# PSUM banks of layer 0 in a four-batch transformer kernel: three for the first keys and values, one for the second int8 block

## The chip, the cores and the metric

The kernel runs on one core of a Trainium2 chip as one launch. The metric is the device time of that launch in microseconds. The core has five engines, each with its own in-order instruction queue: TensorE (PE), VectorE (DVE), ScalarE (ACT), GpSimd (POOL) and SyncE (SP). Matrix products land in PSUM, which this kernel cuts into eight banks, "bank0" to "bank7", each one tile of 128 partitions by 512 float32 values.

## The reference, cut to what matters

The input `x` has 4 batches of 512 rows by 512 columns. Four residual steps follow one another; layer 0 is the first two:

```
x = x + tanh(g_xattn[0]) * L0_xattn(layernorm(x), fside, ctx)     # int8 block
x = x + tanh(g_ffn[0])   * L0_ffn(layernorm(x), w_fc, w_proj)     # ternary block
x = x + tanh(g_xattn[1]) * L1_xattn(layernorm(x), ctx, mask, Wq, Wk, Wv, Wo)
x = x + tanh(g_ffn[1])   * L1_ffn(layernorm(x), router_w, norm_w, gate_w, up_w, down_w)
```

The int8 block is a small expert network for each batch, with both its products in a smoothed int8 form:

```
s   = sqrt(max(amax_x, EPS) / max(amax_w, EPS))    # amax per column
x_q = round((x / s) / x_scale), w_q = round((w * s) / w_scale)    # scale per row: max / 127
out = x_q @ w_q.T * x_scale * w_scale.T
h   = smooth_quant_linear(xe, guw);  a = silu(gate) * up;  y = smooth_quant_linear(a, dw)
```

The ternary block is `square(relu(x @ sign(w_fc).T)) @ sign(w_proj).T`, scaled by the mean sizes of the weights, where the signs are taken against a threshold. The attention of layer 1 needs keys and values, `ctx @ Wk` and `ctx @ Wv`, of every batch. They depend on nothing that layer 0 computes, so they can be worked out at any time before.

## The kernel before, in words

All of layer 0 lies in one block of code. The batches are staged like this, in program order: `int8_block(0)`; the means of the ternary weights (`mean_of`); `int8_block(1)`; the signs of the ternary weights (`load_signs`, 22 pieces of which each takes two DVE passes, a transpose on PE and a copy on ACT); `keys_values_of(0)` and `keys_values_of(1)`; `ternary_in(0)`; then for each batch `ternary_block(b)`, with `int8_block(b + 1)` put in at high priority while batches 1 and 2 are in the ternary block, and `keys_values_of(2)` after batch 0's ternary block and `keys_values_of(3)` at the end. This program order is not the order of execution. A scheduler sorts the instructions of each engine by priority and by when it thinks they can start, and what it makes is fixed: every engine then works its list strictly in order. The tag of a tile (here a bank) is another order: the users of one bank follow one another as in the program, whatever their priorities.

The steps that matter here, by their lines:

- `int8_block` (from layer norm on): `column_max` transposes the activations, four 128x128 pieces to a bank (L198), and DVE reduces the bank (L251); four banks for the first product, two for the second. A scale per column follows (L294 and the square root L151 to L158, L296, L298), is turned into rows by PE (L204), copied by ACT (L300), and multiplied in by DVE (L303, activations) and POOL (L305, weights). `quantize` takes row maxima (L275), scales (L281), transposes (L198) and ACT copies each bank out (L283); DVE clips (L284). Then four products of the first matrix (L336), each read by DVE (L340), SiLU (L341) and a product on POOL (L342). The second half does all of this again on half the columns (`weight_max` L264 and L266, then L198 to L284), with four products L350, each read by DVE (L358) and added to the residual by POOL (L359). The maxima of the weights come first of all, by a DVE reduction (L259).
- Every one of those PSUM tiles comes from `home()`, which goes round the banks of `HOMES` for this batch: banks 4 and 5 for batch 0, 6 and 0 for batch 1, bank 0 alone for batches 2 and 3.
- `keys_values` transposes the context (L495, copied by L496), then makes 16 products of 128x512 with two matmuls each (L501). ACT copies each product to one of two staging places (L503), and SP stores it to memory (L504). Its banks are 7 and 3 in turn for batches 0 and 1, and 3 alone for batches 2 and 3.
- `ternary_in` normalises on ACT (L180), transposes (L436) and splits into two parts (L439 on ACT, L440 on DVE). Its tile `xn` shares a ring of two with the tiles `h` and `y` of the int8 blocks.
- `ternary_block` makes 160 matmuls with the first weights (L462) and 160 with the second (L449, into banks 4 to 7), with the two passes L470 and L472 on ACT, L473 on POOL and L474 on DVE between them. Banks 1 and 2 (`turn_bank`) serve the first products, the signs and the transposes.

Of the kernel before, what the change touches and what calls it, by code (L numbers as in the profile page):

```python
# [57 lines left out]
def kernel(  # L58
# [71 lines left out]
    def bank(i, dtype=F32):  # L130

        return bank_p.tile([P, 512], dtype, tag=f"bank{i}", name=f"bank{i}")
# [77 lines left out]
    with tc.tile_pool(name="q8", bufs=1) as q8, tc.tile_pool(name="l0", bufs=2) as l0, tc.tile_pool(  # L210
# [4 lines left out]
        def next_of(what, n):  # L215
            turns[what] += 1
            return turns[what] % n
# [4 lines left out]

        HOMES = ((4, 5), (6, 0), (0,), (0,))
        xlast = X[B - 1].rearrange("p t k -> p (t k)")
        first_room = (place_in(dn, SLOT + 4096, 512), place_in(dn, SLOT + 4608, 1024))
        rooms = [
# [11 lines left out]
        def home():  # L240
            mine = HOMES[now[0]]
            return bank(mine[next_of("home", len(mine))])
# [240 lines left out]
        def load_context(b, queue):  # L483
            at = SLOT + 2048 if b in (0, B - 1) else SLOT
            cr = place_in(dn, at, NT * DC).rearrange("p (t k) -> p t k", t=NT)
            queue.dma_start(cr, rows(cvec[b]))
            return cr

        def keys_values(b, place, cr):

            cT = place_in(dn, SLOT + 1024, KC * S).rearrange("p (k s) -> p k s", k=KC)
            for i in range(KC):
                tp = place()
                for t in range(NT):
                    nc.tensor.transpose(tp[:, t * P : (t + 1) * P], cr[:, t, i * P : (i + 1) * P], ident)  # L495
                nc.scalar.copy(cT[:, i, :], tp)  # L496

            def product(dst, lhs, rhs):
                ps = place()
                for i in range(KC):  # L500
                    nc.tensor.matmul(ps, lhsT=lhs(i), rhs=rhs(i), start=(i == 0), stop=(i == KC - 1))  # L501
                st = place_in(dn, SLOT + 2048 + 512 * next_of("kvs", 2), 512)
                nc.scalar.copy(st, ps)  # L503
                nc.sync.dma_start(dst, st)  # L504

            for j in range(NKV):
                product(
                    kd[b][j * HD : (j + 1) * HD, :],
                    lambda i: wkv[0][:, i, j * HD : (j + 1) * HD],
                    lambda i: cT[:, i, :],  # L510
                )
            for t in range(NT):
                for c in range(0, NKV * HD, 512):
                    product(
                        vd[b][t * P : (t + 1) * P, c : c + 512],
                        lambda i: cT[:, i, t * P : (t + 1) * P],
                        lambda i: wkv[1][:, i, c : c + 512],
                    )
# [8 lines left out]
        fs1 = load_rows(1, nc.gpsimd)  # L527

        def keys_values_of(b):
            places = (7, 3) if b < 2 else (3,)  # L530
            context = load_context(b, nc.sync) if b else ctx0
            keys_values(b, lambda: bank(places[next_of("kv", len(places))]), context)

# [7 lines left out]
        load_signs(w_fc, fcT, NH, KD, fc_thr, held)  # L541
        load_signs(w_proj, pjT, KD, NH, pj_thr)
        keys_values_of(0)
        keys_values_of(1)
        xT = ternary_in(0)
        for b in range(B):
            if 0 < b and b + 1 < B:
                with tc.high_priority(offset=2000):
                    int8_block(b + 1, load_rows(b + 1), load_cross(b + 1))
            ternary_block(b, xT)  # L550
            if b + 1 < B:
                with tc.high_priority(offset=0):
                    xT = ternary_in(b + 1)
            if b == 0:
                keys_values_of(2)
# [562 lines left out]
    for i in range(LAST + 3):  # L1118
        b, n = divmod(i, NHEAD)
# [199 lines left out]
```

## Time and profile before

| | us |
|---|---|
| median of 3 runs (lowest to highest) | 1570.09 (1568.76 to 1570.95) |
| the profiled execution, its own time | 1567.48 |
| its span, first to last instruction | 1565.7 |
| PE, DVE, ACT, POOL busy in the span | 1475.8, 905.0, 554.0, 414.0 |
| first instruction of the first ternary block (L462) | 164.26 after the start of the span |
| PE busy in 0 to 164.26 | 128.43 |
| PE busy in 164.26 to 440 | 255.78 of 275.74 |
| mean granted TensorE clock | 0.988 |

The span leaves out about 1.8 us of the profiled execution's own time. All times inside the kernel are given from the start of the span. The first 440 us or so are layer 0; the rest is attention and the routed experts. In the timeline a line has the start, the length, the engine, the line of the kernel, the operation, output and input with shapes, the number of instructions merged into the line, and in brackets how long the engine was idle before and what released it. One float32 matmul of the program shows as two records on PE, and one keys-or-values product as four.

### The profile page before, as it was taken

How to read it: one execution, taken by the hardware profiler on the slowest of the kernel's cores; microseconds unless marked ns; L12 is line 12 of the kernel's file. 1: busy time of each engine (PE TensorE's matmuls, PEld its weight loads, DVE VectorE, ACT ScalarE, POOL GpSimd, SP SyncE). 2: the span in 40 equal slices, each digit the busy share in tenths (PEclk: the TensorE clock that was granted, in tenths of full speed). 3: DMA queues.
4: the chain of work that ended last, by engine and by line, in shares of the span. 5: the costliest groups of instructions: out<-in, count | busy, mean ns of one | idle time of the engine just before them, and what ended most of it. 6: DMA issues, size and time to landing. Idle time of an engine off the chain costs nothing. (4 is left out here: it accounts for less than half of the span.)

```text
span 1565.7 us, 15898 instructions
## 1 busy us (share of the span) xinstructions
PE 1475.8 (94%) x4294; PEld 740.9 (47%) x4294; DVE 905.0 (58%) x2339; ACT 554.0 (35%) x1141; POOL 414.0 (26%) x540
## 2 busy tenths in 40 slices
PE   4988998899999999999999999999999998899995
PEld 2454656666544444444444444444444443455553
DVE  5898737556275555586565675665668553653320
ACT  3554453444243333253323353333433331412111
POOL 2232314352311113131131141141141111335422
PEclk9999999999999999999999999999999999999998
DMA  8633111013355445475455485475584653567542
GB/s 300 222 116 129 47 41 62 28 41 97 126 160 150 133 138 157 136 218 153 127 151 141 129 223 149 117 187 143 153 233 127 159 146 99 149 115 144 122 89 38
DMA packets 110840, 211.10 MB, mean 135 GB/s; under 512 B 28816, under 2 KB 32912, under 8 KB 110752
## 3 DMA queue, kind: packets, MB, share of 16 engines
q0 software_dynamic: 32736, 97.73, 24.0%
q1 hardware_dynamic: 70224, 100.74, 22.9%
q10 hardware_dynamic: 7792, 11.60, 2.1%
q8 instruction: 37, 0.61, 0.2%
q14 instruction: 51, 0.42, 0.1%
HBM read 95.34 MB, written 34.93 MB: 83 GB/s over the span
## 5 line engine op out<-in xcount | busy, mean ns | idle before, releaser
L674 DVE CUSTOM_DVE_ANT_0 e<-bank,mask_b 128x512 f32<-128x512 f32 x256 | 175.0, 688 | 245.7 <-PE bank L669 245.6
L694 PE MATMUL bank<-eT,v 128*128 128x512 f32 x512 | 230.5, 592 | 2.2 <-DVE nmax L674 2.2
L669 PE MATMUL bank<-kT,qT 128*128 128x512 f32 x512 | 231.1, 593 | 0.0
L708 PE MATMUL bank<-wo,oT 128*128 128x512 f32 x512 | 230.7, 592 | 0.3 <-ACT oT L698 0.3
L677 ACT ACTIVATE e<-e,nmax 128x512 f32<-128x512 f32 x256 | 184.3, 720 | 81.6 <-DVE nmax L674 74.5
L571 DVE STREAM_TRANSPOSE blocks<-e 128x512 f32<-128x512 f32 x256 | 158.9, 677 | 30.7 <-DMA eT<-blocks 26.1
L656 PE MATMUL bank<-gu,wq 128*128 128x512 f32 x384 | 174.9, 594 | 1.2 <-DVE nmax L674 1.2
L694 PEld LDWEIGHTS bank<-eT,v 128*128 128x128 f32 x512 | 97.1, 190 | 125.4 <-issue 109.3
L669 PEld LDWEIGHTS bank<-kT,qT 128*128 128x128 f32 x512 | 97.0, 190 | 123.1 <-issue 114.8
L708 PEld LDWEIGHTS bank<-wo,oT 128*128 128x128 f32 x512 | 97.1, 190 | 122.7 <-issue 120.1
L698 ACT COPY oT<-bank 128x512 f32<-128x512 f32 x64 | 37.4, 584 | 315.9 <-PE bank L694 298.4
L656 PEld LDWEIGHTS bank<-gu,wq 128*128 128x128 f32 x384 | 72.3, 190 | 91.9 <-issue 82.3
L635 POOL DMA_DIRECT2D wq<-in_L_xattn_Wq_dram x64 | 48.5, 758 | 245.8 <-PE bank L656 223.7
L685 DVE TENSOR_SCALAR e<-e,rt 128x512 f32<-128x512 f32 x256 | 108.2, 485 | 2.1
L650 POOL DMA_DIRECT2D wo<-in_L_xattn_Wo_dram x64 | 36.5, 571 | 266.9 <-PE bank L708 260.7
L660 ACT ACTIVATE qT<-bank 128x512 f32<-128x512 f32 x64 | 38.2, 597 | 171.6 <-PE bank L656 165.7
L449 PE MATMUL bank<-pjT,hT 128*128 128x512 f32 x320 | 86.4, 405 | 5.4 <-DVE hT L474 5.4
L462 PE MATMUL bank<-xfT,fcT 128*128 128x512 f32 x320 | 89.8, 410 | 0.0
L1093 PE MATMUL bank<-gu,turned 128*128 x192 | 86.5, 593 | 0.0
L501 PE MATMUL bank<-dn,gu 128*128 128x512 f32 x128 | 68.9, 655 | 10.5 <-ACT dn L503 5.0
L473 POOL TENSOR_TENSOR r<-r 128x512 f32<-128x512 f32 x40 | 41.7, 1044 | 107.8 <-ACT hT L472 83.5
L1093 PEld LDWEIGHTS bank<-gu,turned 128*128 128x128 f32 x192 | 56.4, 295 | 28.0 <-issue 5.7
(361 smaller groups left out, 1896.8 us busy)
## 6 DMA issues: line engine op xcount, KB each, us to landing
eT<-blocks SPq DMA_DIRECT2D x1016, 64.0 KB, 2.6
wq<-in_L_xattn_Wq_dram POOLq DMA_DIRECT2D x64, 256.0 KB, 3.8
wo<-in_L_xattn_Wo_dram POOLq DMA_DIRECT2D x64, 256.0 KB, 3.0
kd<-dn SPq DMA_DIRECT2D x32, 256.0 KB, 2.0
vd<-dn SPq DMA_DIRECT2D x32, 256.0 KB, 2.0
kT<-kd POOLq DMA_DIRECT2D x32, 256.0 KB, 3.6
v<-vd POOLq DMA_DIRECT2D x32, 256.0 KB, 4.1
turned<-blocks SPq DMA_DIRECT2D x96, 64.0 KB, 3.5
```

What stands on the lines that cost most here:

```text
L449: nc.tensor.matmul(outs[t], lhsT=h[:, t * P : (t + 1) * P], rhs=pjT[:, j, :], start=(j == 0 and u == 0), stop=(j == NH - 1 and u == 1),)
L462: nc.tensor.matmul(ps, lhsT=fcT[:, i, j * P : (j + 1) * P], rhs=xT[u][:, i, :], start=(u == 0 and i == 0), stop=(u == 1 and i == KD - 1),)
L501: nc.tensor.matmul(ps, lhsT=lhs(i), rhs=rhs(i), start=(i == 0), stop=(i == KC - 1))
L571: nc.vector.transpose(blocks[:, :, :, t, :].rearrange("p c s r -> p s c r"), src.rearrange("p (s c i) -> p s c i", c=NQ, i=Q))
L656: nc.tensor.matmul(ps, lhsT=th[:, i, :], rhs=xT[:, :, i, :], start=(i == 0), stop=(i == KD - 1))
L669: nc.tensor.matmul(ps, lhsT=qT[:, t * P : (t + 1) * P], rhs=kT, start=True, stop=True)
L674: nc.vector.tensor_tensor_reduce(e, ps, mask_b[b], -1.0, 3.0e38, ALU.add, ALU.min, nmax[:, t : t + 1])
L677: nc.scalar.activation(e, e, AF.Exp, bias=nmax[:, t : t + 1], scale=-1.0, accum_out=total[:, t : t + 1])
L685: nc.vector.tensor_scalar(es[:, t, :], es[:, t, :], rt[:, t : t + 1], None, ALU.mult)
L694: nc.tensor.matmul(ps, lhsT=v[:, s, :], rhs=eT[:, :, s, :], start=(s == 0), stop=(s == NT - 1))
L708: nc.tensor.matmul(sums[b][t], lhsT=oT[:, t * P : (t + 1) * P], rhs=to, start=(n == 0), stop=(n == NHEAD - 1))
L1093: nc.tensor.matmul(ps, lhsT=xgT[k], rhs=gu[:, bass.ds(e, 1), k, :], start=(k == 0), stop=(k == KD - 1))
```

## The change

Two lines. The second int8 block (batch 1) keeps bank 6 and gives up bank 0, so that each of its PSUM tiles waits until the one before it has been read. The keys and values of batches 0 and 1 go round the banks 7, 3 and 0. Batches 2 and 3 are as before in both places.

```diff
-        HOMES = ((4, 5), (6, 0), (0,), (0,))
+        HOMES = ((4, 5), (6,), (0,), (0,))
...
         def keys_values_of(b):
-            places = (7, 3) if b < 2 else (3,)
+            places = (7, 3, 0) if b < 2 else (3,)
             context = load_context(b, nc.sync) if b else ctx0
             keys_values(b, lambda: bank(places[next_of("kv", len(places))]), context)
```

No instruction is added to the arithmetic or taken from it. The scheduler, which sees other waits, puts the lists of PE, DVE, ACT, POOL and SP in another order up to the end of layer 0. Before the first L462 on PE there are now 92 matmuls of line L501 where there were 79; the counts of the int8 blocks, the signs and `ternary_in(0)` before it are the same. On ACT two more loads of an activation table stand in that stretch (another L151 and another L341).

## The prediction

> **What bounds the kernel now.** I read the page's busy slices first, then busy time by stage, then the instruction timeline around the stage where the ternary blocks start, then the waits of PE, and last the built instruction lists of both programs. From the page:
>
> ```profile
> PE   4988998899999999999999999999999998899995
> DVE  5898737556275555586565675665668553653320
> ```
>
> A slice is 39.1 us. From the fifth slice on PE is the full engine and DVE is half idle: there, time is PE work plus PE's gaps. In slices 2 to 4 DVE is as full as PE. By stage (length; busy time and records of PE, PEld, DVE, ACT, POOL; clock, DMA share, GB/s):
>
> ```profile
> 20.00:60.00 40.00, 33.23 (x122) 17.64 (x123) 33.23 (x78) 23.64 (x52) 13.06 (x27) 0.91 0.75 258
> 60.00:100.00 40.00, 37.34 (x165) 19.53 (x164) 38.68 (x79) 19.72 (x37) 13.79 (x14) 1.00 0.47 165
> 100.00:140.00 40.00, 33.25 (x160) 17.75 (x159) 34.81 (x76) 22.86 (x44) 9.98 (x12) 0.96 0.35 126
> 140.00:164.26 24.26, 20.63 (x78) 10.08 (x77) 18.98 (x48) 11.54 (x22) 5.14 (x5) 1.00 0.37 131
> 164.26:440.00 275.74, 255.78 (x1074) 171.76 (x1073) 152.64 (x342) 111.26 (x197) 97.15 (x110) 0.99 0.20 64
> ```
>
> Between 20 and 164.26 PE is idle 144.3 - 124.5 = 19.8 us and DVE 144.3 - 125.7 = 18.6 us. What ends this stage is read from the timeline:
>
> ```profile
> 154.68 0.73 DVE L358 SCALAR_TENSOR_TENSOR y<-bank,gsc,xlast 128x512 f32<-128x512 f32 x1
> 155.50 1.27 POOL L359 TENSOR_TENSOR gu<-gu,y 128x512 f32<-128x512 f32 x1 [2.19 <-DVE fs_am L267]
> 156.80 0.81 ACT L180 ACTIVATE xn<-gu,ln_d,ln_rstd 128x512 f32<-128x512 f32 x1 [2.14 <-POOL gu L359]
> 164.26 3.08 PE L462 MATMUL bank<-xfT,fcT 128*128 128x512 f32 x11
> ```
>
> The last y of int8 block 1 releases a buffer on POOL, ACT waits for it (xn shares the ring), and 7.5 us after the second xn the ternary block starts. So **the end of int8 block 1 sets when the PE-bound part begins**; keys and values only fill PE before it.
>
> **The change, part by part.**
>
> *The third bank of keys and values.* Its worth is what PE waits there. PE's waits from 20 to 138 us, where keys and values 0 and 1 lie:
>
> ```profile
> PE bank L264 <- DVE dn L259: 3.4, 1, 3.4
> ...
> PE bank L501 <- ACT dn L503: 1.3, 1, 1.3
> ```
>
> The Trainium skill (page "Perfetto Trace Analysis", section "Matmuls") says that independent matmul groups should rotate through PSUM banks so that emptying one overlaps the next group. Taken by that rule the 32 products would have 32 copies of 0.585 us (L503's mean) to hide, 18.7 us; by the row at most 1.3 us is left unhidden by two banks. The row decides: 0 to 1.3 us. The same rule speaks against the other half of the change, and there the rows agree with it (below). Two staging places and one ACT copy per product stay as they are, so products do not come faster than these.
>
> *What moves.* In the lists of the changed program 92 L501 matmuls instead of 79 stand before the first L462. Thirteen at 1.02 us (two records in the timeline, 1.02 each time) are 13.3 us of PE work taken out of the PE-bound part. If the first L462 kept its time, the kernel would be 13.3 us faster; it breaks even if L462 comes 13.3 us later, at 177.6. On SP the loads of batch 3 (fside L316, context L323, x L318) move behind four to seven more stores; nothing reads them before those products are made, so I take 0, with one exception in step 4. Behind the waiting L316 three stores are queued, and through the two staging places ACT's next copies: they cover two products, so 0 to 2 us, taken as 0. POOL's list has the same order up to the first L473.
>
> *The one bank of block 1.* The nearest row is block 2, which has one bank already, against block 1 with two, in the ACT copies L283:
>
> ```profile
> 111.45 1.13 ACT L283 ACTIVATE wT<-bank 128x512 bf16<-128x512 f32 x2
> 113.43 1.08 ACT L283 ACTIVATE wT<-bank 128x512 bf16<-128x512 f32 x2 [0.37 <-PE bank L198]
> 198.73 0.60 ACT L283 ACTIVATE wT<-bank 128x512 bf16<-128x512 f32 x1 [0.75 <-PE bank L198]
> 200.09 0.60 ACT L283 ACTIVATE wT<-bank 128x512 bf16<-128x512 f32 x1 [0.77 <-PE bank L198]
> ```
>
> With one bank a copy comes every 1.36 to 1.7 us, (201.47 - 191.19)/7 = 1.47; with two, eight take 7.0 us. Behind each now stands whatever L501 half the list has next (1.02). Following block 1 down the new DVE list with durations of this trace, its own places against before:
>
> 1. Column maxima: four L251, each waiting for the transpose of a bank that the one before it frees, with L414 and L417 between: up_q (L294) about 81 instead of 75.1, +6.
> 2. The row copy L300 of block 1 (before at 80.12) now stands on ACT behind block 0's L283s and L311, near 94. POOL's L305 of block 1 (4.95 us for four) runs 95 to 100, and block 0's L359 is behind it; block 0's third y on DVE waits for that L359 (ring of two), about 4 us with all of DVE's list behind it. Then the L303s, L275 (2.28 twice), L259 (1.93) and eight L281: the last L281 ends near 117 instead of 107.3, +10.
> 3. Eight L283 on one bank with L501 halves between: the clip L284 of wT at about 131 instead of 114.8, +16. The sign passes cover this on DVE; they are used up by it.
> 4. Four L336 and L340 on one bank. The list puts block 3's L259, 3.69 us in this trace, between the first and the second L340. Its load waits on SP until block 1's wT is transposed, so it may be later still. First L340 near 134 (116.8), fourth near 143.6 (124.3), +19.
> 5. The second half took 125.0 to 154.7, 29.7 us. Taken out: sign passes 5.3 us and an L259 of 3.7. Put in: 0.9 for the second L251, 0.8 for the second row, about 4 for four L283, 3 for four L350/L358 ("PE bank L350 <- DVE y L358: 3.2" is block 2's wait for the same), and L501 halves in front, some 4 us. About 33: last y near 177, +22.
>
> Then 7.5 to 8 us as before: the first L462 near 186, +22. The two extra table loads on ACT (1.28 us each in this trace) fall inside step 4 and 5 waits: 0 to 2.6, taken as 0.
>
> *What is late next.* PE-bound time loses 13.3 us of L501 that filled 212 to 240 us:
>
> ```profile
> 180.00:200.00 20.00, 0.00 (x0) 0.00 (x0) 1.00 0.00 0
> 220.00:240.00 20.00, 14.03 (x28) 4.67 (x28) 1.00 0.24 92
> ```
>
> (L501 alone, PE busy first.) At 212 to 224 they stand beside ternary_in(1), where L462 of batch 1 waits for xT until 219.8; with four halves, two L336 groups and the transposes left, PE stays covered there. Later, ternary block 1 is 13 us shorter while int8 blocks 2 and 3 keep their latency on bank 0, so PE can wait at the ends of ternary blocks 1 and 2, as it does now at 287.6 ("PE bank L449 <- DVE hT L474: 5.4, 3, 3.7"). In the new list keys and values 3 fill the second of these. I take +2, between 0 and 6.
>
> **Sum.** +22 - 13.3 + 2 = about +10 (the third bank's 1.3 is inside the rounding). Against the profiled execution's own 1567.5 (span 1565.7 and 1.8 around it) that is 1577.5; this execution is 2.6 below the median 1570.1, so against the median it is 1580.
>
> Bounds: step by step the +22 could be 14 (an L501 half in front of each block-1 step overlaps its wait fully in steps 3 and 5, -8) or 27 (block 3's L259 held by its load, POOL order worse, +5); the moved work is worth 10 to 13.3; the later gaps 0 to 6. That gives +1 to +20 or so around +10.
>
> **The rivals.**
>
> - *Faster: the first L462 slips less than the work that was put before it.* PE has 19.8 us of idle before 164.26, room for 13.3. Mechanism: block 1's longer waits are all inside the DVE idle (18.6 us) and the sign passes, so the chain above is shorter than counted one by one. It decides at 177.6: with L462 at 171 the kernel is 171 - 164.3 - 13.3 = -6.6, 1563.5. For it: the sum of work before L462 is the same on DVE. Against: steps 2 and 4 put DVE itself in waits with its list blocked behind. Chance 0.16.
> - *No difference.* L462 between about 174 and 181 with nothing lost later: 1570. That also covers the case that one bank costs little because block 1 is already spaced by DVE. Chance 0.12.
> - *Slower as worked out*, 1573 to 1588: chance 0.60.
> - *Slower by more*: the fill for the ends of the ternary blocks is gone and block 3's tail on bank 0 comes to stand before ternary_in(3); another 8 us, 1588 and above. For it: the new list puts block 3's last part behind the last L449 of ternary block 2. Against: keys and values 3 lie beside it. Chance 0.12.
> - That the change does not do what it says, for the keys and values: most likely true in effect; at the same place in the list they are one product ahead. It is part of all cases.
>
> **The numbers.** Slower by over 0.2% (3.1 us, about what a measurement of this kernel can tell from no change) 0.72, within 0.12, faster 0.16. The likeliest is 1580. The range 1568 to 1593 leaves out most of the faster case and the far end of the last.
>
> **What would show it.** After: L462 first near 186 and above 177.6; 26 more L501 records before it; the four L340 of block 1 with an L259 of 3.7 us among them, the fourth near 143; L283 of block 1 one at a time, 1.5 us or more apart; an idle of about 4 us on DVE before an L358 with POOL L359 as releaser near 100; L501 waiting for L503 before 138 for under 1.3 us. I am wrong if the first L462 is before 174, or if PE's idle between it and 440 falls by several us instead of rising.

## The result, and the profile after

The changed kernel takes 1576.94 us (median of 9 runs, 1572.42 to 1578.66); the kernel before, run beside it on the same chip, takes 1567.55 us (9 runs). The ratio is 1.0060, 95% interval 1.0045 to 1.0074: the change costs about 9.4 us. The prediction was +10 us, 1580.

The busy slices of the page, after. The slices are now 39.4 us long:

```profile
PE   5888899898999999999999999999999998899995
DVE  5786656766265556585565575665668552553220
```

The two kernels differ mainly in slices 2 to 5. The same by stage, after, with the boundary at its own first L462 (columns as for before: length; busy time and records of PE, PEld, DVE, ACT, POOL; granted clock, DMA share, GB/s):

```profile
20.00:60.00 40.00, 31.81 (x100) 16.46 (x100) 29.48 (x62) 20.81 (x46) 12.71 (x26) 0.91 0.70 249
60.00:100.00 40.00, 36.68 (x185) 20.82 (x187) 35.92 (x89) 22.99 (x45) 12.14 (x14) 1.00 0.46 161
100.00:140.00 40.00, 33.42 (x143) 17.77 (x143) 33.94 (x61) 20.92 (x39) 6.95 (x8) 0.88 0.42 139
140.00:184.59 44.59, 36.10 (x118) 15.97 (x117) 25.37 (x72) 20.06 (x35) 9.26 (x10) 0.99 0.31 112
184.59:440.00 255.41, 233.38 (x1019) 163.37 (x1024) 147.33 (x320) 102.81 (x179) 93.80 (x107) 0.99 0.17 56
```

From 20 us to the first L462, DVE is now idle 164.6 - 124.7 = 39.9 us where it was idle 18.6: it waits longer, it does not work longer. PE does 13.6 us more there, the thirteen L501 that its list had added, and is idle 26.6 us instead of 19.8.

The timeline of after, along block 1's path:

```profile
82.59 0.16 DVE L294 SCALAR_TENSOR_TENSOR up_q<-up_am,fs_am 128x4 f32<-128x4 f32 x1
...
100.54 0.75 DVE L358 SCALAR_TENSOR_TENSOR y<-bank,gsc,dn 128x512 f32<-128x512 f32 x1 [2.94 <-POOL gu L359]
...
133.01 3.70 DVE L259 TENSOR_REDUCE dn<-gu 128x512 f32<-128x2048 f32 x1
...
139.46 0.75 DVE L340 SCALAR_TENSOR_TENSOR h<-bank,upa_sc,xlast 128x512 f32<-128x512 f32 x1 [1.89 <-PE bank L336]
...
175.88 0.73 DVE L358 SCALAR_TENSOR_TENSOR y<-bank,gsc,xlast 128x512 f32<-128x512 f32 x1
...
184.59 2.36 PE L462 MATMUL bank<-xfT,fcT 128*128 128x512 f32 x9
```

The last y of block 1 starts 21.2 us later than before (154.68) and the first L462 20.3 us later (164.26). Why the steps between are slow shows in ACT's timeline of after, with three of block 1's copies (L283) on its single bank:

```profile
122.05 0.60 ACT L283 ACTIVATE wT<-bank 128x512 bf16<-128x512 f32 x1 [0.40 <-PE bank L198]
...
123.23 0.59 ACT L503 COPY dn<-bank 128x512 f32<-128x512 f32 x1
123.72 0.60 ACT L283 ACTIVATE wT<-bank 128x512 bf16<-128x512 f32 x1
...
125.09 0.60 ACT L283 ACTIVATE wT<-bank 128x512 bf16<-128x512 f32 x1 [0.51 <-PE bank L198]
```

A copy of 0.60 us comes every 1.3 to 1.9 us (one gap of 2.3 us aside). Before, they came in pairs of 1.1 us. The next transposes may start only when the copy has emptied the bank, but PE does not stand idle for it; its list has other work there:

```profile
122.08 1.08 PE L501 MATMUL bank<-gu,dn 128*128 128x512 f32 x2
122.99 0.60 PE L198 MATMUL bank<-ident,gu 128*128 128x128 f32 x4
123.43 0.28 PE L422 MATMUL bank<-ident_b,dn 128*128 128x128 bf16 x2
123.54 1.08 PE L501 MATMUL bank<-gu,dn 128*128 128x512 f32 x2
124.45 0.60 PE L198 MATMUL bank<-ident,gu 128*128 128x128 f32 x4
```

Before, two banks of transposes followed each other (eight pieces in a line):

```profile
109.29 1.04 PE L198 MATMUL bank<-ident,dn 128*128 128x128 f32 x8
...
110.68 1.15 PE L198 MATMUL bank<-ident,gu 128*128 128x128 f32 x8
```

With one bank the transposes at 122.99 and 124.45 have the copy of 123.72 to 124.32 between them, and an L501 fills the time. In the seven gaps of these eight copies the next transposes start 0.06 to 0.86 us after the copy has ended, 2.7 us in all: about so much the filler can have added here, and the rest is the way of a group through its bank. From block 1's last L281 (the end of its first scaling) to its last y, PE is busy 53.2 of 62.0 us after and 42.2 of 48.0 us before, with 35 L501 in the stretch instead of 25: the longer stretch is mostly filled, not idle.

How 20.3 us at the first L462 become 10.6 us at the end of the span, from the starts of L462 and of layer 1's queries (L656) in both traces. The L501 matmuls of a stretch are counted in PE's lists, before to after:

| stretch | before, us | after, us | difference | L501 in it |
|---|---|---|---|---|
| up to the first L462 | 164.3 | 184.6 | +20.3 | 79 to 92 |
| first to last L462 (ternary blocks) | 235.8 | 230.7 | -5.1 | 31 to 25 |
| to the first L656 | 10.1 | 9.2 | -0.9 | 4 to 3 |
| first to last L656 | 874.2 | 867.6 | -6.6 | 14 to 8 |
| to the end | 281.3 | 284.2 | +2.9 | none |

The thirteen L501 that moved ahead come back as 5.1 + 0.9 + 6.6 = 12.6 us, but only half of that in the ternary blocks; the other half is work that before ran past the start of layer 1. The last row has no edited code in it; over all the profiles here it varies from 281 to 289 us with no order, so it is taken as scatter. In what follows times are judged by the ratios, not by single spans.

### The profile page after: what moved, and what is told of

Same layout as the page of the kernel before. It is cut to its first block, busy times and chain, and to the rows that moved or that the text cites. A ratio compares the mean times of both kernels' runs of the same rounds, so it can differ in the third digit from the quotient of the medians.

```text
span 1576.3 us, 15894 instructions
## 1 busy us (share of the span) xinstructions
PE 1478.9 (94%) x4285; PEld 743.9 (47%) x4294; DVE 905.7 (57%) x2339; ACT 558.1 (35%) x1143; POOL 412.6 (26%) x540
## 5 line engine op out<-in xcount | busy, mean ns | idle before, releaser
L708 PE MATMUL bank<-wo,oT 128*128 128x512 f32 x512 | 230.7, 592 | 0.3 <-ACT oT L698 0.3
L656 PE MATMUL bank<-gu,wq 128*128 128x512 f32 x384 | 174.4, 594 | 1.2 <-DVE nmax L674 1.2
L669 PEld LDWEIGHTS bank<-kT,qT 128*128 128x128 f32 x512 | 97.1, 190 | 122.9 <-issue 115.3
L656 PEld LDWEIGHTS bank<-gu,wq 128*128 128x128 f32 x384 | 72.3, 190 | 91.9 <-issue 81.6
L449 PE MATMUL bank<-pjT,hT 128*128 128x512 f32 x320 | 88.4, 407 | 2.5 <-DVE hT L474 2.5
L462 PE MATMUL bank<-xfT,fcT 128*128 128x512 f32 x320 | 89.5, 410 | 0.0
L501 PE MATMUL bank<-dn,gu 128*128 128x512 f32 x128 | 65.2, 627 | 11.4 <-ACT dn L503 6.0
L501 PE MATMUL bank<-gu,dn 128*128 128x512 f32 x128 | 68.3, 637 | 5.5 <-ACT dn L503 5.5
L1215 PE MATMUL bank<-dn,hidT 128*128 x144 | 69.2, 604 | 1.4 <-DVE hidT L1189 1.4
```

The lines of the kernel that those rows point to most:

```text
L449: nc.tensor.matmul(outs[t], lhsT=h[:, t * P : (t + 1) * P], rhs=pjT[:, j, :], start=(j == 0 and u == 0), stop=(j == NH - 1 and u == 1),)
L462: nc.tensor.matmul(ps, lhsT=fcT[:, i, j * P : (j + 1) * P], rhs=xT[u][:, i, :], start=(u == 0 and i == 0), stop=(u == 1 and i == KD - 1),)
L656: nc.tensor.matmul(ps, lhsT=th[:, i, :], rhs=xT[:, :, i, :], start=(i == 0), stop=(i == KD - 1))
L669: nc.tensor.matmul(ps, lhsT=qT[:, t * P : (t + 1) * P], rhs=kT, start=True, stop=True)
L708: nc.tensor.matmul(sums[b][t], lhsT=oT[:, t * P : (t + 1) * P], rhs=to, start=(n == 0), stop=(n == NHEAD - 1))
```

## The experiments

Each was timed in five rounds beside the kernel before; the edits are shown without the lines that only keep a name for an instruction. The table has its path in the profile, in us: the start of up_q (L294), the end of the last L281 of block 1's first product, the end of its last y (L358), the start of the first L462; then the L501 matmuls ahead of that, and the ratio with its interval.

| kernel | up_q | last L281 | last y | first L462 | L501 | ratio |
|---|---|---|---|---|---|---|
| before | 75.1 | 107.4 | 155.4 | 164.3 | 79 | 1 |
| after | 82.6 | 114.6 | 176.6 | 184.6 | 92 | 1.0060 (1.0045-1.0074) |
| e1_one_bank | 79.8 | 114.3 | 174.2 | 182.1 | 90 | 1.0043 (1.0032-1.0055) |
| e2_third_bank | 75.2 | 109.4 | 155.2 | 219.2 | 64 | 1.0389 (1.0363-1.0415) |
| e9_late_two | 84.3 | 116.3 | 164.2 | 175.2 | 81 | 1.0072 (1.0047-1.0098) |
| e5_kv_one_bank | 73.1 | 105.0 | 165.6 | 173.4 | 74 | 1.0093 (1.0073-1.0114) |
| e4_no_l259_between | 81.0 | 113.0 | 173.0 | 182.8 | 90 | 1.0050 (1.0033-1.0067) |
| e11_pool_order | 81.9 | 115.3 | 177.6 | 186.7 | 92 | 1.0061 (1.0041-1.0081) |
| e18_row_first | 81.6 | 113.7 | 175.6 | 184.8 | 92 | 1.0041 (1.0026-1.0056) |
| e12_third_after_early | 75.6 | 108.7 | 149.8 | 158.6 | 71 | 1.0067 (1.0045-1.0089) |
| e13_six_five | 74.7 | 107.7 | 150.6 | 161.6 | 79 | 0.9978 (0.9967-0.9989) |
| e19_both_repairs | 81.4 | 113.5 | 157.2 | 166.1 | 79 | 0.9999 (0.9987-1.0011) |
| e14_l259_behind | 79.0 | 112.1 | 154.1 | 164.5 | 77 | 1.0069 (1.0052-1.0086) |
| e16_three_late | 75.3 | 108.4 | 144.8 | 164.5 | 76 | 1.0061 (1.0040-1.0083) |

### The two halves apart

The kernel before, with only block 1's bank taken away:

```diff
-        HOMES = ((4, 5), (6, 0), (0,), (0,))
+        HOMES = ((4, 5), (6,), (0,), (0,))
```

> Half of the change alone: int8 block 1 on bank 6 alone, keys and values of batches 0 and 1 on banks 7 and 3 as before. 90 L501 matmuls stand before the first L462 (before 79, after 92). Main theory (the lone bank of block 1 is the whole cost; time = before + slip of the first L462 - 1.02 us for each L501 moved ahead of it): L462 at 183 to 186 (before 164.3, after 184.6), so +19 to +22 less 11.2, time +8 to +10, ratio 1.005 to 1.0065, the same as the full change. Rival 1 (the extra keys and values in front of block 1's steps, let in by their third bank, are the cost): L462 below 175, ratio under 1.002. Rival 2 (the third bank earns several us): slower than the full change by 3 us or more, ratio over 1.008.

L462 at 182.1 and a ratio of 1.0043. The interval overlaps that of the full change, and the path is the same within 3 us at every point. This half is the change's cost, and the 90 L501 ahead of L462 come with it: the third bank is not what moved them. The two extra table loads on ACT are absent here (7 up to the first L462, as before; 9 after), so the cost does not hang on them either.

The other half alone:

```diff
-            places = (7, 3) if b < 2 else (3,)
+            places = (7, 3, 0) if b < 2 else (3,)
```

> The other half alone: keys and values on banks 7, 3 and 0, block 1 keeps 6 and 0. Bank 0's users follow one another as in the program, so the first product on bank 0 stands behind block 1's last use of it; only 64 L501 matmuls stand before the first L462 (before 79). Main theory: block 1 ends no later than before, L462 at 158 to 165, and 15 L501 (15.3 us) go back into the PE-bound part: time +9 to +15, ratio 1.006 to 1.010. Rival (the third bank lets PE run ahead and earns its wait of about 1.3 us): ratio 0.998 to 1.000. Rival (the L501 were only filling idle time and their place does not matter): ratio within 1.002 with L462 near 160.

A wide miss: +61 us. Block 1 did end as before (155.2), but L462 came at 219.2. PE's timeline has two lone L501 matmuls (four records) near the start, the last at 23.60, and then no other until block 1 is done:

```profile
23.60 1.92 PE L501 MATMUL bank<-dn,gu 128*128 128x512 f32 x2
...
154.00 0.67 PE L495 MATMUL bank<-ident,dn 128*128 128x128 f32 x4 [0.88 <-DVE y L358]
157.00 13.96 PE L501 MATMUL bank<-dn,gu 128*128 128x512 f32 x28
...
219.16 1.40 PE L462 MATMUL bank<-xfT,fcT 128*128 128x512 f32 x5
```

The second context transpose (L495) falls on bank 0, and the users of a bank follow one another as in the program, where block 1 comes before the keys and values. So it waited for block 1's last use of that bank, the third y (which ended at 153.94), and all 62 L501 behind it then ran on the path of the ternary block. I had counted how many were ahead of L462 and not when they could run. Two things follow. Bank 0 can serve the keys and values from the start only if block 1 gives it up: the halves of the change cannot be judged as independent edits. And with no keys and values beside it on PE, block 1 ends just 0.2 us earlier than before. That does not show that the filler costs it nothing: PE's granted clock was lower in this run (last section), and eight of block 1's L198 take 1.97 us there at 107.12, against 1.04 before. The two effects were not separated.

### Where the slip is made

The full change, with a second bank for block 1 from its first L283 on, when block 0 is done with bank 5:

```diff
         def quantize(src, kt, dst, tag):
+            if now[0] == 1:
+                HOMES[1] = (6, 5)
```

> The full change, but block 1 gets bank 5 beside 6 from its first L283 on (block 0 is done with bank 5 by then); its column maxima and row copies of the first product stay on bank 6 alone. 81 L501 matmuls before the first L462. Main theory (slip made at steps 1 and 2, about 7 us at the last L281 of the first product, and 13 more at the L283s, L340s and L358s on one bank): L462 at 171 to 176, time +7 to +12 less 2, so +5 to +10, ratio 1.003 to 1.006: the slip halves but the time hardly falls, since eleven fewer L501 are moved ahead. Rival 1 (the slip is made wholly by the one bank from the L283s on): L462 at 164 to 167, ratio 0.999 to 1.001. Rival 2 (the slip is made wholly before, by the list order): L462 at 182 or more, ratio over 1.009.

L462 at 175.2, as expected. ACT's copies come in pairs again:

```profile
116.44 1.24 ACT L283 ACTIVATE aT<-bank 128x512 bf16<-128x512 f32 x2 [2.33 <-PE bank L198]
119.00 1.09 ACT L283 ACTIVATE aT<-bank 128x512 bf16<-128x512 f32 x2
120.44 1.13 ACT L283 ACTIVATE wT<-bank 128x512 bf16<-128x512 f32 x2
122.30 1.08 ACT L283 ACTIVATE wT<-bank 128x512 bf16<-128x512 f32 x2 [0.47 <-PE bank L198]
```

From the last L281 to the last y it takes 47.9 us; before took 48.0, after 62.0. **The lone bank, with the list that goes with it, costs 14 us between these two points**, and the rest of the slip is there before them. The list changes with the bank (22 L501 in the stretch here, 35 in the full change), so what one bank would cost without filler is not known. Yet the time did not fall (1.0072): L462 is 9.4 us earlier than in the full change, and eleven L501 fewer (11.2 us) stand ahead of it.

Keys and values on one bank, block 1 on one bank:

```diff
-            places = (7, 3, 0) if b < 2 else (3,)
+            places = (7,) if b < 2 else (3,)
```

> Block 1 on bank 6 alone as in the full change, and keys and values of batches 0 and 1 on bank 7 alone, so that each product waits for the copy of the one before. 74, 29, 3, 22 L501 in the four stretches. Theory (end of block 1 and filler placed before it set the time): fewer L501 in front of block 1's steps, L462 at 178 to 184 (full change 184.6), but five fewer before it than in the kernel before instead of thirteen more, time +18 to +24, ratio 1.011 to 1.015; L501 waits for L503 of 15 us or more up to 138. Rival (the bank count of keys and values does not matter, since two staging places and one ACT copy per product set their pace): ratio as the full change, 1.004 to 1.007, and no more waits for L503 than there (4.8 us from 20 to 185).

The expected waits for L503 did not come: 7.0 us up to 138 us, not 15 (1.3 to 3.1 in the kernels with two banks for the first two batches, 1.6 to 2.6 in those with three, the third-bank run left out). The scheduler put fewer products into that stretch, 27 instead of 32, and eighteen L501 fewer than in the full change stand ahead of L462, which is why the kernel is slower all the same. DVE's timeline holds the surprise:

```profile
61.99 0.69 DVE L251 TENSOR_REDUCE up_am<-bank 128x1 f32<-128x512 f32 x1
63.91 0.68 DVE L251 TENSOR_REDUCE up_am<-bank 128x1 f32<-128x512 f32 x1
64.61 3.72 DVE L259 TENSOR_REDUCE dn<-gu 128x512 f32<-128x2048 f32 x1
...
73.07 0.15 DVE L294 SCALAR_TENSOR_TENSOR up_q<-up_am,fs_am 128x4 f32<-128x4 f32 x1
```

Block 1 has one bank here too, and up_q is 2.0 us earlier than before, not 7.5 later. Two of its column maxima (L251) stand ahead of the long L259 in DVE's list; before it was one, in the full change none. In the full change the L259 itself ended 3.3 us later than before (74.6 to 71.3), with block 0's L340s late ahead of it, and then the column maxima came about 2 us apart, 8.0 us from the L259's end to up_q instead of 3.8. So the first part of the slip is 3.3 us made in block 0 and 4.2 us behind the L259, and another list takes away both. The bank alone is not shown as the cause of either: e14 below has two banks for these maxima and its L259 ends at 75.2; the third-bank run has two banks as well and takes 7.3 us from the L259 to up_q (at its low clock), with all four maxima behind it as in the full change. From up_q to the last L281 it takes 31.9 us here, 32.3 before, 32.0 after: nothing is added in that stretch in any of them. From the last L281 to the last y it takes 60.6 us, the lone bank's price again.

### Waits on the way, removed one at a time

In the full change, DVE's third y of block 0 waits 2.94 us for POOL, which has block 1's L305 first. This kernel makes those L305 depend on block 0's L359:

```diff
+                if now[0] == 1 and kt == KD: tc.add_manual_dep(it.ins, adds[0].ins.name, mybir.DependencyInfo(mybir.DependencyClass.Sync, mybir.DependencyReason.DATA), reason="behind block 0")
```

> The full change, with block 1's four L305 of the first product (5.2 us on POOL) put behind block 0's four L359, so that DVE's third y no longer waits for them (2.94 us idle in the full change). 92 L501 before the first L462, as in the full change, and the same list on PE. Theory of the prediction's step 2 (that idle is lost time, with all of DVE's list behind it): last L281 of block 1's first product 3 us earlier, first L462 at 181 to 182, time 3 us below the full change, ratio to before 1.002 to 1.004. Rival (L305 now runs 101 to 106 instead of 94 to 99, and the weights' maxima L275 wait for it instead: the row copy L300 that came late is what holds both): first L462 184 to 186, time as the full change, ratio 1.004 to 1.007.

The same 92 L501, the wait cut to 0.72 us, and nothing gained (L462 at 186.7). DVE's and POOL's timeline (L305 is L304 in this kernel):

```profile
96.20 0.75 DVE L358 SCALAR_TENSOR_TENSOR y<-bank,gsc,dn 128x512 f32<-128x512 f32 x1 [0.72 <-POOL gu L359]
...
99.93 4.96 POOL L304 TENSOR_TENSOR gu<-gu,xlast 128x512 f32<-128x512 f32 x4
...
104.93 2.29 DVE L275 TENSOR_REDUCE upw_mx<-gu 128x4 f32<-128x2048 f32 x1 [4.36 <-POOL gu L304]
```

The 2.9 us have turned into 4.4 us in front of the weights' maxima: the two POOL groups are needed in either order before DVE can go on.

The weight maxima of block 3 (L259) put behind block 1's last y:

```diff
+            if now[0] == 3: tc.add_manual_dep(first.ins, ys[1].ins.name, mybir.DependencyInfo(mybir.DependencyClass.Sync, mybir.DependencyReason.DATA), reason="behind block 1")
```

> The full change, with the weight maxima of block 3 (L259, 3.70 us, between the first and the second L340 of block 1) held behind block 1's last y; nothing else asked for. 90 L501 matmuls before the first L462. Main theory (DVE's list is blocked by it and block 1 waits 3.7 us): L462 near 181, fourth L340 near 138, time 2 to 4 us below the full change, ratio to before 1.003 to 1.005. Rival (the one bank's own waits cover it: without it the same time goes into waiting for L336 and L501): L462 stays 183 to 185, time as the full change, ratio 1.005 to 1.0075. Rival (held back, it delays block 3 in turn): ratio over 1.008.

Block 1's fourth L340 came 4.2 us earlier (137.54 instead of 141.71) and its last y 3.6 us, but L462 only 1.8 us: the L259 (173.0 to 176.7) now stands in front of the four L440 of the ternary input in DVE's list, and PE waits 1.60 us for the first of them. The ratio is that of the full change within the intervals.

The copy of block 1's row (L300) ahead of block 0's last four L283 on ACT:

```diff
+            if now[0] == 1 and kt == KD:
+                for c in copies[0][-4:]: tc.add_manual_dep(c.ins, row_copy.ins.name, mybir.DependencyInfo(mybir.DependencyClass.Sync, mybir.DependencyReason.DATA), reason="behind the row")
```

> The full change, with ACT's four L283 of block 0's second product put behind the row copy L300 of block 1 (93.4 us in the full change, 80.1 before, 78.1 where keys and values had one bank); banks as in the full change. L501 in the four stretches 92, 25, 3, 8, as in the full change. Theory (the place of this one copy on ACT's list makes the slip of the first part, and the one bank from the L283s on makes the other 13 us): last L281 of block 1's first product at 106 to 109 (full change 114.6), first L462 at 177 to 180, time before + 13 to 16 - 13.3 + 2, so +2 to +5, ratio 1.001 to 1.003. Rival (as with the order on POOL, the next thing in the list takes its place): L462 over 183, ratio 1.004 to 1.007.

The last L281 came at 113.7, not at 106 to 109. The copy moved less than I had asked for, from 93.39 to 91.53, since four L503 still stand ahead of it:

```profile
91.53 0.59 ACT L300 COPY xlast<-bank 128x512 f32<-128x512 f32 x1
```

So this says little about the copy itself. With up_q at 81.6, the last L281 is again 32.1 us after it.

### What the third bank is worth, and a better kernel

The kernel before with block 1 on banks 6 and 0 up to its first L283 and on 6 and 5 after that:

```diff
-        HOMES = ((4, 5), (6, 0), (0,), (0,))
+        HOMES = [(4, 5), (6, 0), (0,), (0,)]
...
         def quantize(src, kt, dst, tag):
+            if now[0] == 1:
+                HOMES[1] = (6, 5)
```

> The kernel before, with block 1 on banks 6 and 0 up to its first L283 and on 6 and 5 from there; keys and values on 7 and 3. Counts of L501 as before (79, 31, 4, 14). It is what the run with the third bank from batch 1 on is compared with. Main theory (which second bank it is does not matter): L462 within 1.5 us of 164.3, ratio 0.999 to 1.001. Rival (bank 5 comes free from block 0 too late): L462 over 167, ratio over 1.002.

It is faster than the kernel before, 0.9978 (0.9967 to 0.9989), some 3.5 us, and so beats both kernels. I had expected no difference. The L501 counts are those of before in every stretch; the last y ends 4.8 us earlier and L462 comes 2.7 us earlier:

```profile
149.21 1.40 DVE L358 SCALAR_TENSOR_TENSOR y<-bank,gsc,xlast 128x512 f32<-128x512 f32 x2
...
161.59 3.07 PE L462 MATMUL bank<-xfT,fcT 128*128 128x512 f32 x11
```

Most of it is there by the last L340, which ends 4.2 us earlier. Why bank 5 is better for it than bank 0 was not taken apart.

The same, with bank 0 as the third bank for the keys and values of batch 1:

```diff
-            places = (7, 3) if b < 2 else (3,)
+            places = ((7, 3), (7, 3, 0), (3,), (3,))[b]
```

> The third bank without the loss of block 1's second: block 1 on banks 6 and 0 up to its first L283, on 6 and 5 from there; keys and values of batch 0 on 7 and 3, of batch 1 on 7, 3 and 0. L501 before the first L462 / up to the last L462 / up to the first L656 / after it: 71, 30, 3, 24 (before 79, 31, 4, 14). Main theory (a third bank is worth at most 1.3 us, and what counts is the end of block 1 and how much filler stands before it): L462 at 158 to 164, eight L501 more to make later, time +3 to +8, ratio 1.002 to 1.005. Rival (the third bank was worth more, the full change only hid it): ratio under 0.999.

Slower than the run above by about 14 us (0.0089 of 1567.5), though L462 is 3.0 us earlier: eight L501 fewer stand ahead of it, and 24 instead of 14 are left for layer 1, where the stretch from the first to the last L656 takes 884.4 us instead of 870.6. Ten L501 are 10.2 us of that. The waits for L503 up to 138 us are 1.8 us, with two banks 1.7. The third bank brought nothing here either.

The full change with both repairs, the row copy first and a second bank for block 1 from its first L283 on:

> The same, and block 1 on banks 6 and 5 from its first L283 on; keys and values on 7, 3 and 0 throughout. L501 79, 31, 4, 14, exactly as in the kernel before. Theory (these two are the whole slip, and the third bank of keys and values is worth nothing): first L462 at 161 to 167, ratio 0.997 to 1.002, as the kernel with 6 and 0, then 6 and 5 (0.998). Rival (the third bank is worth several us once block 1 does not suffer): ratio under 0.996. Rival (some of the slip is made elsewhere): L462 over 170, ratio over 1.004.

0.9999, with the L501 counts of the kernel before (79, 31, 4, 14) and L462 at 166.1. So with three banks for keys and values throughout, the kernel is as fast as before once these two things are put right, and no faster. Against e18, which lacks only the second bank, the way from the last L281 to the last y falls from 61.9 to 43.7 us: in this list the bank is worth 18 us, in e9's 14. Against e9, which lacks only the row copy's order, L462 is 9.1 us earlier, though in e18 that order alone did not move L462. The two edits make a new list together; their gains do not add up one by one.

Two attempts to gain more on e13_six_five. Block 3's L259 behind the first split of the second ternary input:

```diff
+            if now[0] == 3 and kt == KD: tc.add_manual_dep(first.ins, parts[0].ins.name, mybir.DependencyInfo(mybir.DependencyClass.Sync, mybir.DependencyReason.DATA), reason="behind the first parts")
```

> Block 1 on banks 6 and 0, then 6 and 5; keys and values on 7 and 3; and block 3's L259 (3.7 us on DVE) held behind the first split of the second ternary input, so out of block 1's stretch altogether. L501 77, 28, 3, 20 (before 79, 31, 4, 14). Theory: L462 at 157 to 160 (161.6 without this), less 2 L501, time 3 to 6 us below the kernel before, ratio 0.996 to 0.998. Rival (the six L501 more in layer 1 and a later block 3 take it back, as with the third bank from batch 1 on, which lost 8 us more than its L462 told): ratio 0.999 to 1.005.

And on top of that, three banks for block 1 from its first L283 on:

```diff
-                HOMES[1] = (6, 5)
+                HOMES[1] = (6, 5, 4)
```

> As the run before it, but block 1 on banks 6, 5 and 4 from its first L283 on. L501 76, 29, 3, 20. Theory (two banks hide the copies, a third adds little): L462 within 3 us of that run, ratio within 0.001 of it. Rival (the waits for banks left with two, such as 0.4 us before the second y, were still on the path): L462 at 153 to 156, ratio 0.994 to 0.996.

Both are slower than before (1.0069, 1.0061). The second is instructive: the last y ended at 144.8, 10.6 us earlier than before, but L462 came at 164.5. Its timeline:

```profile
144.03 0.74 DVE L358 SCALAR_TENSOR_TENSOR y<-bank,gsc,xlast 128x512 f32<-128x512 f32 x1
...
145.31 7.81 SPq L504 DMA_DIRECT2D kd<-dn  x3
...
152.19 0.59 ACT L503 COPY dn<-bank 128x512 f32<-128x512 f32 x1 [5.33 <-DMA kd<-dn]
152.68 1.52 ACT L180 ACTIVATE xn<-gu,ln_d,ln_rstd 128x512 f32<-128x512 f32 x2
```

ACT waited 5.33 us for a store to empty a staging place, with the normalisation L180 of the ternary input behind it. So at this place the store is the next bound. From the last y to L462 it takes 19.7 us instead of 8.8; some 6 us of the difference is this wait, and behind it block 2's transposes and maxima (L198, L251) stand among the steps of the ternary input. The rest of the loss lies later: from the first L462 to the first L656 PE is idle 26.9 us in e14 and 25.2 in e16, 19.4 before. What it waits for there was not taken apart.

## Why the prediction was right

**The sum.** +22 - 13.3 + 2 was predicted; +20.3 at L462, -12.6 returned, and +9.4 by the ratio were measured. The two measured terms make 7.7, inside the ratio's interval (7.1 to 11.6 us). The balance was worked out rightly; that the sum came within 1 us is in part luck, since the slip and the last term were both put somewhat too high. The rule behind it, time = slip of the first L462 less 1.02 us for each L501 moved ahead, gives after +7.0, e1 +6.6, e4 +7.3, e18 +7.2, e11 +9.1, e9 +8.9, e5 +14.2, e13 -2.7, e19 +1.8, and the ratios (times 1567.5 us) say +9.4, +6.7, +7.8, +6.4, +9.6, +11.3, +14.6, -3.4 and -0.2. It holds within 2.5 us for these. It comes out 6 to 9 us too low for e12, e14 and e16, and 9 us too high for the third bank alone (+70 against +61): what is lost or gained after the first L462 is not in it. For e14 and e16 it is mostly the longer idle of PE named above (7.5 and 5.8 us more than before); for the other two it stays open. The prediction's upper bound, by its own terms, is 27 - 10 + 6 = +23, which is the end of its range, and not +20.

**Step 1** (up_q +6, from column maxima that wait for each other's bank): near in size, +7.5, but 3.3 of it was made in block 0, which the step had kept at its old times, and 4.2 behind the L259, where bank and list were not separated.

**Step 2** (row copy on ACT, POOL's order, 4 us of idle, last L281 +10): wrong in its size. Each event was there, at its place: the row copy at 93.4, L305 from 94.1 to 99.3, 3.4 us of idle before the third and fourth y. But the slip did not grow, +7.5 at up_q and +7.2 at the last L281. DVE is idle 4.8 us between these two points after and 0.7 before, as the step had it, but it has only 27.2 us of work there instead of 31.6: 2.0 us of sign passes and 2.5 of other work now stand outside. The step added an idle and kept the work as it was; and when the idle was taken away, DVE waited elsewhere instead.

**Steps 3 to 5** (+12 more up to the last y) came out near: 14.0, and it goes when the bank is given back. wT's clip came at 129.1 (131 predicted), the first and fourth L340 at 131.8 and 141.7 (134, 143.6) with L259 between the first two, the second half took 33.4 us (33), the last y came at 175.9 (177). Some L283 came 1.34 us apart, closer than the 1.5 given as the sign. Step 4's L259 was a real block for the L340s, but moving it gained only 1.8 us at L462: it came back before L440.

**The third bank** was put at 0 to 1.3 us from the waits of PE. The waits for L503 up to 138 us did not even fall. PE's waits of after, from 20 to 138 us:

```profile
PE bank L501 <- ACT dn L503: 2.6, 2, 1.3
```

They were 1.3 us with two banks. The rule of the Trainium skill (page "Perfetto Trace Analysis", section "Matmuls"), that independent groups should rotate through the banks, would have given an estimate of 18.7 us for the keys and values, with all 32 copies of 0.585 us left in the open; even the run with one bank instead of two had only 5.7 us more of these waits, for 27 products. For block 1 the rule holds: 14 us. As the lists have it, the difference is what waits behind: PE has other work beside the keys and values, while the steps of block 1 follow one another through its bank.

**What is late next** was put too high (+2) and in the wrong place. The waits of L449 for hT, which I expected to grow, fell from 5.4 to 2.5 us. Of the 13.3 us moved ahead 12.6 came back, so 0.7 was lost; from the first L462 to the first L656 PE is idle 20.2 us after and 19.4 before. Up to 440 us, the mark that the prediction gave, its idle rose from 20.0 to 22.0 us.

## What to carry to other kernels

Count a bank from what waits for it: on a chain that other engines follow step by step, the second bank was worth 14 to 18 us; for filler that PE can leave and come back to, the third was worth nothing that could be measured. Work moved ahead of a stage is a gain only as far as the stage does not slip with it, so take both from the trace and subtract. And before counting an idle as lost, ask what the same engine needs next: in the one case tried here it came from the same busy engine, and the idle only moved.

## What the runs showed of the hardware

The granted TensorE clock was lower where PE did less. In the third-bank run PE was busy for half of the early stretches, and its windows read:

```profile
20.00:60.00 40.00, 19.86 (x93) 14.34 (x95) 34.78 (x80) 20.81 (x44) 13.37 (x27) 0.70 0.61 219
60.00:100.00 40.00, 19.38 (x95) 12.66 (x94) 32.46 (x74) 10.69 (x21) 15.61 (x16) 0.65 0.14 47
100.00:140.00 40.00, 19.77 (x113) 13.44 (x114) 36.01 (x76) 16.48 (x32) 4.89 (x8) 0.63 0.18 59
```

The clock was 0.63 to 0.70 there (the figure after POOL's), and 0.91 to 1.00 in the same three windows of the kernel before, where PE was busy 33 to 37 us of each 40. In this pair of runs the filler thus went with a higher clock. What that is worth to block 1 is not shown: it ended at the same time in both (155.2 and 155.4), but one run lacks the filler and has the lower clock, and the other has both filler and clock.
